# Layer 0's scatter: rows and running sums by TensorE products in place of VectorE scans, the mask by GpSimd alone, and a first pair of products from the upper rows

## The chip, the cores and the metric

The kernel runs on one core of a Trainium2 chip. The metric is the device time of one execution in microseconds. Before the change it is 974.45 us (median of three runs, 974.11 to 974.66). The engines are TensorE (PE; its weight loads are PEld), VectorE (DVE), ScalarE (ACT), GpSimd (POOL) and SyncE (SP), which issues the transfers.

## What is computed

Four graph layers follow each other on `x` of 32 x 512 x 128, with one 512 x 512 matrix `adj`. Each layer takes `h = max(layernorm(x), 0)` and adds its result to `x`. Layer 0, cut to what matters:

```python
h0 = einsum('bnf,fg->bng', input, W[0]);  h1 = einsum('bnf,fg->bng', input, W[1])
m = adj > 0
idx = cumsum(m.reshape(-1).astype(int32)) - 1
vals = e[0][idx].reshape(adj.shape)        # e has 256 entries: an index past them reads the last
A = softmax(where(m, vals, NEG), axis=1)
out = einsum('ij,bjg->big', A * M, h0) + einsum('ij,bjg->big', A * (1 - M), h1) + bias   # M = eye
```

So the first 256 positive places of `adj`, counted row by row, get their own value of `e`, and all later ones the last value. Layer 1 multiplies `h` by `adj` in several hops, layer 2 by `adj * adj`, layer 3 is an attention masked by `adj`:

```python
A = exp(tanh(Q @ K.T / sqrt(D) / 8) * 8) * A_shape;  out = (A / A.sum(-1)) @ x @ v     # A_shape = adj
```

## The kernel before

Rows are in four blocks of 128 (`NT` = 4). The 256 positions of `e` lie on the partitions in two blocks (`NK` = 2). A preparation finds, for each of the 256, its row and column, scatters their values into a 512 x 512 score by TensorE, and makes `att`, the softmax. `q` counts pairs of batches (16 of them), `r` rounds of two pairs.

```python
# ... loads: adj, x(0), x(1), w0, ecol, elast, x(2..7), b0, qw, kw, x(8..15), the rest: all issued by SyncE
for t in range(NT):                                   # mask and its row counts
    nc.vector.tensor_scalar(m[:, t, :], adj_s[:, t, :], 0.0, None, OP.is_gt, OP.add, accum_out=rc[:, t : t + 1])
for t in range(NT):                                   # 0 where there is an edge, NEG elsewhere
    nc.gpsimd.tensor_scalar(att[:, t, :], m[:, t, :], -1.0, -NEG, OP.add, OP.mult)
# ... adj transposed by 16 TensorE transposes, copied by ScalarE, stored to adjT_d for layer 3
# ... pi: number of edges up to and with each row; pc: the same, along the free axis (products with upto)
for t in range(NT):                                   # of_row[row, k]: is position k in this row?
    nc.vector.tensor_scalar(s, cols[:, :NE], incl[:, t : t + 1], None, OP.is_lt)
    nc.vector.scalar_tensor_tensor(of_row[:, t, :], cols[:, :NE], before[:, t : t + 1], s, OP.is_ge, OP.mult)
    for kk in range(NK):                              # pg: the mask row of each position
        nc.tensor.matmul(pg[kk], of_row[:, t, blk(kk)], m[:, t, :], ...)
# ... pb: edges before that row; keep_busy(6) above and keep_busy(18) here: products whose result nobody reads
for kk in range(NK):                                  # row of each position
    nc.vector.tensor_scalar(s, pc, rows[:, kk : kk + 1], None, OP.is_le, OP.add, accum_out=row_of[:, kk : kk + 1])
# ... statistics of pairs 0 and 1; ScalarE writes m * (-elast) to us[t], GpSimd adds it to att
for kk in range(NK):                                  # column of each position
    nc.vector.tensor_tensor_scan(w, pg[kk], zero.to_broadcast([P, N]), bk[:, kk : kk + 1], OP.add, OP.add)
    nc.vector.tensor_scalar(s, w, rows[:, kk : kk + 1], None, OP.is_le, OP.add, accum_out=col_of[:, kk : kk + 1])
# ... at_row, at_col, at_part: 0/1 and value matrices made from row_of and col_of by VectorE
def score_rows(t):                                    # 8 products of 512 columns per block of rows
    ...
def softmax_rows(t):
    nc.vector.scalar_tensor_tensor(u, ph, elastn, att[:, t, :], OP.mult, OP.add)
    nc.vector.tensor_tensor_reduce(u, pv, u, 1.0, 3.0e38, OP.add, OP.min, least[:, t : t + 1])
    nc.scalar.activation(u, u, AF.Exp, bias=least[:, t : t + 1], scale=-1.0, accum_out=total[:, t : t + 1])
def scaled_rows(t, u):
    nc.vector.reciprocal(total[:, t : t + 1], total[:, t : t + 1])
    nc.scalar.mul(split(att[:, t, :]), crossed(u), total[:, t : t + 1])
    # ... GpSimd takes the diagonal out of att into diag
# ... att transposed by TensorE (16 of 128 x 128), copied whole into attT, sums of its quarters for the products
```

The products of layer 0 use seven half-size products per pair in place of eight (banks `a`, `c`, `d`; `u` holds partial sums; `rt_g` and `sums_att` are the sums that they need):

```python
ORDER = ((1, "a", True), (6, "c", True), (5, "d", True), (7, "c", False), (2, "a", False),
         (4, "c", False), (3, "d", False))
```

In round `r` TensorE also makes the projections `p_g` of the pairs of the next round, from `hT`, the normed input with features on the partitions. For pairs 0 to 3 `hT` comes from TensorE transposes. From pair 4 on it goes through memory: VectorE transposes 32 x 32 blocks into `hb`, four stores bring them to `d`, one load brings `hT` back.

```python
def turn_steps(h, name, done):
    for b in range(2):
        nc.vector.transpose(hb[:, :, b].rearrange(...), h[:, b].rearrange(...))
        yield
    for i in range(NQR):
        nc.sync.dma_start(d[:, :, i, :].rearrange("j c e -> c j e"), hb[i * QR : (i + 1) * QR].rearrange(...))
    nc.sync.dma_start(hT.rearrange("p i b n -> p (i b n)"), d.rearrange("j c i e -> (j c) (i e)"))
```

Up to the end of layer 0 TensorE, VectorE, ScalarE and GpSimd run their instructions in the order of the source (`tc.manual_schedule`). SyncE isn't among the engines named there, and after layer 0 a scheduler orders all of them.

Of the kernel before, what the change touches and what calls it, by code (L numbers as in the profile page):

```python
# [24 lines left out]
def kernel(  # L25
# [95 lines left out]
    def load_rows(ap, name):  # L121
        o = ap.shape[0] // P
        w = const.tile([P, o, ap.shape[1]], F32, name=name)
        nc.sync.dma_start(w, ap.rearrange("(o f) g -> f o g", f=P))
        return w
# [9 lines left out]
    load_x(0)  # L135
    load_x(1)
    w0 = const.tile([P, 2, D], F32, name="w0")
    nc.sync.dma_start(w0, w_l0.rearrange("o f g -> f o g"))
    ecol = const.tile([P, NK], F32, name="ecol")
    nc.sync.dma_start(ecol, e_l0.rearrange("o (k p) -> p (o k)", p=P))  # L140
    elast = const.tile([P, 1], F32, name="elast")
    nc.sync.dma_start(elast, bass.AP(tensor=e_l0.tensor, offset=e_l0.offset + NE - 1, ap=[[0, P], [1, 1]]))
    for b in range(2, 8):
        load_x(b)
    b0 = load_bcast(bias_l0, "b0")
    qw = load_rows(q_w, "qw")[:, 0, :]
    kw = load_rows(k_w, "kw")[:, 0, :]
    for b in range(8, B // 2):
        load_x(b)
# [32 lines left out]
    zero = const.tile([P, 1], F32, name="zero")  # L182
    nc.vector.memset(zero, 0.0)
# [13 lines left out]
    def stats_steps(q, powers=False):  # L197
# [11 lines left out]
        if powers:  # L209
            nc.gpsimd.tensor_scalar(sd, st[:, :, :, 2], 1.0 / D, EPS, OP.mult, OP.add)  # L210
            nc.gpsimd.tensor_tensor(rs, sd, minus_half, OP.pow)
            nc.gpsimd.tensor_mul(sh, st[:, :, :, 1], rs)
            nc.gpsimd.tensor_scalar(sh, sh, -1.0, None, OP.mult)
        else:
            nc.scalar.activation(sd, st[:, :, :, 2], AF.Sqrt, bias=eps, scale=1.0 / D)
            yield
            nc.vector.reciprocal(rs, sd)
            nc.vector.scalar_tensor_tensor(sh, st[:, :, :, 1], -1.0, rs, OP.mult, OP.mult)  # L218
        shift[q] = sh.rearrange("p k e -> p (k e)")
        scale[q] = rs.rearrange("p k e -> p (k e)")  # L220
        if powers:
            yield
# [22 lines left out]
    def pe_steps(h, name, hT, copy=nc.scalar.copy):  # L245
        ps = [bank(f"p_{name}_{b}") for b in range(2)]
        for b in range(2):
            for t in range(NT):
                nc.tensor.transpose(ps[b][:, blk(t)], h[:, b, t, :], ident)
        yield  # L250
        for b, p in enumerate(ps):
            copy(hT[:, :, b, :].rearrange("p b (a c) -> p b a c", c=QR), crossed(p))
# [40 lines left out]

    def att_sums():
# [5 lines left out]
        sums["att"] = {1: a11, 2: a12, 3: s4, 4: a22, 5: s1, 6: s2, 7: a21}  # L300
        for out, p, bank_of, half, first in ((s1, a21, 2, 1, False), (s2, s1, 0, 0, False),
                                             (a21, a21, 0, 0, True), (s4, s2, 2, 0, True)):
            for k in range(2):
                b = pt[bank_of + k][:, half * H : half * H + H]
                if out is s1:
                    nc.vector.tensor_add(out[:, k], b, p[:, k])
                elif first:
                    nc.vector.tensor_sub(out[:, k], b, p[:, k])
                else:
                    nc.vector.tensor_sub(out[:, k], p[:, k], b)  # L310

# [24 lines left out]
    def products(name, form, left, right, evict):  # L336

        banks = {}
        for k, g, first in ORDER:
# [79 lines left out]
    def project_steps(q, hT, copy=nc.scalar.copy):  # L419
# [9 lines left out]
        for b in range(2):  # L429
            copy(g[r][:, :, b, w, :], pg[b])  # L430

# [14 lines left out]
    adjT = last.tile([P, NT, N], F32, tag="x", name="adjT")  # L446
# [4 lines left out]

    m = prep.tile([P, NT, N], BF16, name="m")
    rc = prep.tile([P, NT], F32, name="rc")
    for t in range(NT):
        nc.vector.tensor_scalar(m[:, t, :], adj_s[:, t, :], 0.0, None, OP.is_gt, OP.add,
                                accum_out=rc[:, t : t + 1])
    rch = prep.tile([P, NT], F16, name="rch")
    nc.vector.tensor_copy(rch, rc)


    att = square_tile("att")
    for t in range(NT):
        nc.gpsimd.tensor_scalar(att[:, t, :], m[:, t, :], -1.0, -NEG, OP.add, OP.mult)
    pt = [bank(f"p_adjT_{j}") for j in range(NT)]
    for t in range(NT):
        transpose_rows(pt, adj_s, t)
    for j in range(NT):
        nc.scalar.copy(adjT[:, j, :], pt[j])
    adjT_d = bounce.tile([N, N], F32, tag="adjT", name="adjT_d", bufs=1)
    nc.sync.dma_start(adjT_d.rearrange("(t p) w -> p t w", p=P), adjT)  # L470
# [6 lines left out]


    pi = bank("p_incl")
    for t in range(NT):  # L480
        for s in range(t + 1):
            nc.tensor.matmul(pi[:, t : t + 1], upto[:, s, blk(t)], rch[:, s : s + 1],
                             start=(s == 0), stop=(s == t))
    pc = bank("p_count")
    for t in range(NT):
        nc.tensor.matmul(pc, rch[:, t : t + 1].to_broadcast([P, P]), upto[:, t, :],
                         start=(t == 0), stop=(t == NT - 1))
    incl = prep.tile([P, NT], F32, name="incl")
    nc.vector.tensor_copy(incl, pi[:, :NT])
    before = prep.tile([P, NT], F32, name="before")  # L490
    nc.vector.tensor_sub(before, incl, rc)
    befh = prep.tile([P, NT], BF16, name="befh")
    nc.vector.tensor_scalar(befh, before, float(NE), None, OP.min)
    keep_busy(6)

    of_row = prep.tile([P, NT, NE], BF16, name="of_row")
    pb = bank("p_before")
    pg = [bank(f"p_row_{kk}") for kk in range(NK)]
    for t in range(NT):
        s = prep.tile([P, NE], F16, tag="lt", name=f"lt_{t}", bufs=2)  # L500
        nc.vector.tensor_scalar(s, cols[:, :NE], incl[:, t : t + 1], None, OP.is_lt)
        nc.vector.scalar_tensor_tensor(of_row[:, t, :], cols[:, :NE], before[:, t : t + 1], s,
                                       OP.is_ge, OP.mult)
        for kk in range(NK):
            nc.tensor.matmul(pg[kk], of_row[:, t, blk(kk)], m[:, t, :], start=(t == 0), stop=(t == NT - 1))
    for kk in range(NK):
        for t in range(NT):
            nc.tensor.matmul(pb[:, kk : kk + 1], of_row[:, t, blk(kk)], befh[:, t : t + 1],
                             start=(t == 0), stop=(t == NT - 1))
    keep_busy(18)  # L510
    row_of = prep.tile([P, NK], F32, name="row_of")
    col_of = prep.tile([P, NK], F32, name="col_of")
    at_row = prep.tile([P, NK, N], BF16, name="at_row")
    at_col = prep.tile([P, NK, N], BF16, name="at_col")
    at_part = prep.tile([P, 3, NK, N], BF16, name="at_part")

# [12 lines left out]
    elastn = prep.tile([P, 1], F32, name="elastn")  # L529
    nc.gpsimd.tensor_scalar(elastn, elast, -1.0, None, OP.mult)  # L530
    us = [prep.tile([P, N], F32, tag="u", name=f"u_{t}", bufs=NT) for t in range(NT)]

    def value(t):
        nc.scalar.mul(us[t], m[:, t, :], elastn)

    def entries(t):
        nc.gpsimd.tensor_add(att[:, t, :], us[t], att[:, t, :])

    value(0)
    value(1)  # L540
    for kk in range(NK):
        s = prep.tile([P, N], F16, tag="scr", name=f"scr_r{kk}", bufs=2)
        nc.vector.tensor_scalar(s, pc, rows[:, kk : kk + 1], None, OP.is_le, OP.add,
                                accum_out=row_of[:, kk : kk + 1])
    ln = [stats_steps(q, powers=q < 2) for q in range(4)]
    go(ln[0])
    entries(0)
    entries(1)
    go(ln[1])
    bk = prep.tile([P, NK], F32, name="bk")  # L550
    nc.vector.tensor_copy(bk, pb[:, :NK])
    for kk in range(NK):
        w = prep.tile([P, N], F32, tag="scan", name=f"scan_{kk}", bufs=1)
        nc.vector.tensor_tensor_scan(w, pg[kk], zero.to_broadcast([P, N]), bk[:, kk : kk + 1], OP.add, OP.add)
        s = prep.tile([P, N], F16, tag="scr", name=f"scr_c{kk}", bufs=2)
        nc.vector.tensor_scalar(s, w, rows[:, kk : kk + 1], None, OP.is_le, OP.add,
                                accum_out=col_of[:, kk : kk + 1])
    h = {q: normed_tile(q) for q in range(3)}
    hT = {q: feature_major(f"hT0_{q}") for q in range(4)}
    normal = [normed_steps(q, h[q]) for q in range(3)]  # L560
    copies = [nc.scalar.copy, nc.vector.tensor_copy, nc.scalar.copy]
    turned = [pe_steps(h[q], f"hT0_{q}", hT[q], copies[q]) for q in range(3)]
    project = [project_steps(q, hT[q], copies[q]) for q in range(3)]
    go(normal[0])
    next(turned[0])
    next(turned[0], None)
# [6 lines left out]
    go(normal[1], 2)  # L573
    value(2)
    value(3)
    entries(2)
    entries(3)
    go(normal[1])
# [42 lines left out]
    for t in range(NT):  # L621
        score_rows(t)
# [499 lines left out]
```

## Time and profile before

| | |
|---|---|
| time, median of 3 | 974.45 us |
| span of the profiled execution | 972.7 us |
| granted TensorE clock, mean | 0.999 |
| first product of layer 0 (`p_l_a`) starts | 37.25 us |
| round 1 starts (next `p_l_a`) | 59.95 us |
| round 2 starts | 79.18 us |
| DMA, mean over the span | 88 GB/s |

Times within the profile count from the first instruction of the span. A line of a group or of the timeline names the source line, the engine, the operation, and the tiles as out<-in, buffer numbers left out. What an engine waited for is shown as waiter <- releaser, with its total time, the number of waits and the longest. The page's own line of the granted clock, in forty slices of 24.3 us (tenths of full speed; 9 is 90% or more), reads:

```profile
PEclk9999999999999999999999999999999999999999
```

It is a mean over each slice, so a short stretch at a lower clock does not show in it.

### The profile page before, as it was taken

The page shows a single profiled execution, that of the slowest core. Times are in us where ns is not written, and L with a number is a line of the kernel's source. Part 1 is how long each engine was busy: PE and PEld are TensorE (multiplying, and loading weights), DVE is VectorE, ACT ScalarE, POOL GpSimd, SP SyncE. Part 2 cuts the span into 40 slices and gives each one's busy share as a digit, 9 for nine tenths or more (in the row PEclk, how much of TensorE's full clock was granted, in tenths as well). Part 3 has the DMA queues.
Part 4 walks back from the last instruction along what each step waited for, and adds up shares of the span by engine and source line. Part 5 has one row for each costly group of instructions (what it writes and reads, how often), then busy time and mean ns, then how long its engine had stood idle before and what let it go on. Part 6 is the DMA issues. An engine that isn't in the chain of part 4 may idle for free.

```text
span 972.7 us, 15180 instructions
## 1 busy us (share of the span) xinstructions
PE 959.0 (99%) x5474; PEld 781.9 (80%) x5474; DVE 581.0 (60%) x1316; ACT 474.6 (49%) x1058; POOL 436.5 (45%) x478
## 2 busy tenths in 40 slices
PE   7999999999999999999999999999999999999998
PEld 4799999898989989889887777777676777777776
DVE  7778896746446545646667756656554444454444
ACT  4874552452242242376628544455674455544553
POOL 5786998842436632531524443334142333223322
PEclk9999999999999999999999999999999999999999
DMA  9145643252421212344233332332131121121111
GB/s 258 52 130 152 192 112 109 66 131 65 129 88 50 82 53 57 109 109 105 71 109 109 108 87 67 87 87 75 55 91 64 44 76 55 56 75 44 55 33 44
DMA packets 82330, 86.04 MB, mean 88 GB/s; under 512 B 6737, under 2 KB 72529, under 8 KB 82257
## 3 DMA queue, kind: packets, MB, share of 16 engines
q1 hardware_dynamic: 82256, 85.09, 31.4%
q8 instruction: 43, 0.70, 0.3%
q14 instruction: 31, 0.25, 0.1%
HBM read 44.17 MB, written 40.89 MB: 87 GB/s over the span
## 4 chain that ended last, share of the span: by engine, by line
PE 91%; DVE 4%; ACT 2%; DMA 2%; SPq 1%; issue 0%; POOL 0%; DVEq 0%; ACTq 0%
PE p_av L1043 12%; PE p_score L1028 11%; PE p_l_c L356 9%; PE p_l_a L356 6%; PE p_l_d L356 6%; PE p_w L405 5%; PE p_msgT_c L349 4%; PE p_x1T_c L349 4%; PE p_feat L405 3%; PE p_hv L405 3%; PE p_msgT_d L349 3%; PE p_msgT_a L349 3%; PE p_qkh L1015 3%; PE p_l L405 3%; PE p_g L405 3%; PE p_phi L998 3%
## 5 line engine op out<-in xcount | busy, mean ns | idle before, releaser
L231 ACT ACTIVATE h<-x,sh,rs 128x128 f32<-128x128 f32 x512 | 208.9, 484 | 56.8 <-DVE sh L218 24.9
L1033 POOL TENSOR_TENSOR ex<-ex,adjTx 128x512 f32<-128x512 f32 x64 | 83.1, 1300 | 206.4 <-ACT ex L1031 206.4
L1029 ACT ACTIVATE ex<-p_score 128x512 f32<-128x512 f32 x128 | 71.9, 587 | 124.5 <-issue 113.0
L1043 PEld LDWEIGHTS p_av<-qkh_hv,ex 128*128 128x128 f32 x1024 | 118.5, 191 | 9.4 <-issue 7.4
L1043 PE MATMUL p_av<-qkh_hv,ex 128*128 128x129 f32 x1024 | 120.1, 275 | 0.8 <-POOL ex L1033 0.8
L1028 PE MATMUL p_score<-qkh_hv,hT 128*128 128x512 f32 x256 | 115.2, 593 | 0.0
L265 DVE STREAM_TRANSPOSE hb_hT<-h 128x512 f32<-128x512 f32 x120 | 81.7, 697 | 33.4 <-ACT h L231 33.1
L1033 DVE TENSOR_TENSOR ex<-ex,adjTx 128x512 f32<-128x512 f32 x64 | 45.4, 709 | 81.8 <-ACT ex L1031 81.8
L203 DVE BATCH_NORM_STATS2 bn<-x 128x6 f32<-128x256 f32 x256 | 92.4, 416 | 0.9
L1028 PEld LDWEIGHTS p_score<-qkh_hv,hT 128*128 128x128 f32 x256 | 46.2, 190 | 46.5 <-issue 45.0
L1031 ACT ACTIVATE ex<-ex 128x512 f32<-128x512 f32 x128 | 76.6, 630 | 1.9
L330 POOL TENSOR_TENSOR rt_feat<-feat,feat 128x256 f32<-128x256 f32 x16 | 11.6, 726 | 137.2 <-ACT feat L982 137.2
L330 POOL TENSOR_TENSOR rt_w<-w 128x512 f32<-128x512 f32 x16 | 20.3, 1268 | 81.5 <-ACT w L889 81.5
L405 PE MATMUL p_w<-th,x1T 128*128 128x128 f32 x256 | 49.5, 275 | 0.0
L405 PE MATMUL p_w<-th,hs 128*128 128x128 f32 x256 | 49.5, 275 | 0.0
L370 ACT COPY x1T<-p_x1T_a 128x256 f32<-128x256 f32 x16 | 5.9, 370 | 84.3 <-PE p_x1T_a L349 84.3
L405 PEld LDWEIGHTS p_hv<-vw,hT 128*128 128x128 f32 x256 | 33.6, 192 | 15.3 <-issue 8.1
L993 POOL TENSOR_TENSOR x<-x,phi2b 128x256 f32<-128x256 f32 x64 | 44.5, 728 | 0.0
L1000 ACT ACTIVATE msgT<-p_phi,phi1b 128x512 f32<-128x512 f32 x32 | 21.7, 678 | 40.7 <-PE p_phi L999 40.7
L666 POOL TENSOR_TENSOR hd<-hT,adiag 128x512 f32<-128x512 f32 x32 | 39.7, 1277 | 1.7 <-ACT adiag L779 1.7
L1048 DVE SCALAR_TENSOR_TENSOR x<-p_av,rsum,x 128x128 f32<-128x128 f32 x128 | 39.1, 347 | 1.9
L982 ACT ACTIVATE feat<-feat 128x512 f32<-128x512 f32 x32 | 20.1, 628 | 40.6 <-DVE feat L981 40.6
(231 smaller groups left out, 2084.0 us busy)
## 6 DMA issues: line engine op xcount, KB each, us to landing
d_hT<-hb_hT SPq DMA_DIRECT2D x240, 128.0 KB
hT<-d_hT SPq DMA_DIRECT2D x60, 512.0 KB
x<-in_x_dram SPq DMA_DIRECT2D x32, 256.0 KB
out_dram<-x SPq DMA_DIRECT2D x31, 256.0 KB
adj_s<-in_adj_dram SPq DMA_DIRECT2D x4, 256.0 KB
adjT_d<-adjT SPq DMA_DIRECT2D x1, 1024.0 KB
sq<-in_adj_dram SPq DMA_DIRECT2D x4, 256.0 KB
adjTx<-adjT_d SPq DMA_DIRECT2D x4, 256.0 KB
```

Source lines behind the costliest of these rows:

```text
L203: nc.vector.bn_stats(st[:, k].rearrange("p e s -> p (e s)"), xt[q][:, b, t : t + 2, :].rearrange("p t f -> p f t"))
L231: nc.scalar.activation(h[:, b, t, :], xt[q][:, b, t, :], AF.Relu, bias=shift[q][:, i : i + 1], scale=scale[q][:, i : i + 1])
L265: nc.vector.transpose(hb[:, :, b].rearrange("p j t r -> p t j r"), h[:, b].rearrange("p t (j c) -> p t j c", c=QR))
L349: nc.tensor.matmul(p[:, :H], b[:, k, :], a[:, k, :], start=(first and k == 0), stop=(k == 1), skip_group_check=True)
L356: nc.tensor.matmul(p[:, i * 2 * D : (i + 1) * 2 * D], a[:, k, blk(i)], b[:, k], start=(first and i == 0 and k == 0), stop=(k == 1), skip_g ...
L405: nc.tensor.matmul(p[:, blk(t)], hT(t), w, start=(i == 0), stop=(i == len(terms) - 1))
L993: tc.keep_in_program_order(nc.gpsimd.tensor_add(xi, xi, spread(phi2b, 2)))
L1028: nc.tensor.matmul(ps, hT[:, t, b, :], qkh, start=True, stop=True)
L1029: nc.scalar.activation(ex[:, t, :], ps, AF.Tanh, scale=1.0 / (8.0 * math.sqrt(D)))
L1031: nc.scalar.activation(ex[:, t, :], ex[:, t, :], AF.Exp, scale=8.0)
L1033: eng.tensor_mul(ex[:, t, :], ex[:, t, :], adjTx[0][:, t, :])
L1043: nc.tensor.matmul(po[:, i, : D + 1], ex[:, t, blk(i0 + i)], hv[:, t, :], start=(t == 0), stop=(t == NT - 1))
```

## The change

It is meant to shorten the preparation ahead of layer 0's first product. Its parts:

- The row of each position comes out of the same small products that give the edges before it (`known` holds, per row, the edges before it and its own number), and the running sum along a row comes from products with the triangular `upto`: first `pgs`, the transposed mask rows, then `pw = pgs x upto`. The two scans and the two counts of rows on VectorE go.
- The mask of the softmax is made by GpSimd in two operations; ScalarE no longer writes `m * (-elast)`.
- `adj` is transposed in 32 x 32 blocks by VectorE in round 1 and stored in that order; layer 3 reads it crossed. TensorE's 16 transposes go.
- `elast`, `ecol`, `qw` and `kw` are loaded by ScalarE's queue, the first four batches of `x` right after `adj`, and the statistics of pairs 0 and 1 are taken in halves.
- In round 0 the order is 1, 2, 6, 5, 7, 4, 3: products 1 and 2 need only rows 0 to 255 of `att`, that is half of each `attT` block, which is copied in halves. The other rows are transposed between them.
- GpSimd scales rows 0 to 2 of the softmax, ScalarE row 3. `keep_busy` is 8, 3, 2, 4 and 1 products instead of 6 and 18.

```diff
+    keep_busy(8)
+    def masked(t):
+        nc.gpsimd.tensor_scalar(att[:, t, :], m[:, t, :], -2.0 * NEG, NEG, OP.mult, OP.add)
+        nc.gpsimd.tensor_scalar(att[:, t, :], att[:, t, :], elastn, None, OP.max)
...
-        for kk in range(NK):
-            nc.tensor.matmul(pg[kk], of_row[:, t, blk(kk)], m[:, t, :], start=(t == 0), stop=(t == NT - 1))
+        for j in range(NT):
+            nc.tensor.matmul(pg[j // 2][:, j % 2, :], m[:, t, blk(j)], of_row[:, t, :], ...)
...
+            nc.tensor.matmul(pb[:, kk, :], of_row[:, t, blk(kk)], known[:, t, :], ...)
+    nc.scalar.copy(pgs[:, 0:2, :], pg[0])
+    nc.vector.tensor_copy(pgs[:, 2:4, :], pg[1])
+    nc.vector.tensor_copy(row_of, pb[:, :, 1])
+    nc.vector.tensor_sub(rest, rows[:, :NK], pb[:, :, 0])
+    for kk in range(NK):
+        for j in range(NT):
+            nc.tensor.matmul(pw[kk][:, j * P :], pgs[:, j, blk(kk)], upto[:, j, j * P :], ...)
...
-        nc.vector.tensor_tensor_scan(w, pg[kk], zero.to_broadcast([P, N]), bk[:, kk : kk + 1], OP.add, OP.add)
-        nc.vector.tensor_scalar(s, w, rows[:, kk : kk + 1], None, OP.is_le, OP.add,
+        nc.vector.tensor_scalar(s, pw[kk], rest[:, kk : kk + 1], None, OP.is_le, OP.add,
                                 accum_out=col_of[:, kk : kk + 1])
...
+    ORDER0 = (ORDER[0], ORDER[4]) + ORDER[1:4] + ORDER[5:]
...
+    def turn_adj():
+        ab = last.tile([P, N // QR, NT, QR], F32, tag="x", name="adj_squares")
+        for t in range(NT):
+            nc.vector.transpose(ab[:, :, t, :], adj_s[:, t, :].rearrange("p (j c) -> p j c", c=QR))
+            yield
+        for b in range(NQR):
+            tc.keep_in_program_order(nc.sync.dma_start(adjT_d[:, blk(b)]..., ab[b * QR : (b + 1) * QR]...))
+        yield
...
             elif i == 1:                       # rounds 1 to 7
                 add(0, 1, 1)
+                if r == 1:
+                    go(squares, 3)
...
             elif i == 4:
+                if r == 1:
+                    go(squares, 3)
...
-                eng.tensor_mul(ex[:, t, :], ex[:, t, :], adjTx[0][:, t, :])
+                eng.tensor_mul(split(ex[:, t, :]), split(ex[:, t, :]), crossed(adjTx[0][:, t, :]))
```

## The prediction

> **What bounds the kernel now.** I read the page's busy times first, then TensorE's waits, then three stretches of the span. Busy times, share of the span, instructions:
>
> ```profile
> PE 959.0 (99%) x5474; PEld 781.9 (80%) x5474; DVE 581.0 (60%) x1316; ACT 474.6 (49%) x1058; POOL 436.5 (45%) x478
> ```
>
> All that TensorE waited for, by its own waits (us in total, times, longest):
>
> ```profile
> PE p_adjT L444 <- DMA adj_s<-in_adj_dram: 4.7, 2, 3.8
> PE p_x1T_c L349 <- DVE x1T L372: 2.5, 7, 0.4
> ```
>
> The stretches are the preparation up to layer 0's first product, round 0, and rounds 1 and 2 (length, then busy time and count of PE, weight load, DVE, ACT, POOL; clock; DMA share; GB/s):
>
> ```profile
> 0.00:37.25 37.25, 31.32 (x171) 18.54 (x171) 28.80 (x83) 22.64 (x48) 22.09 (x44) 1.00 0.73 201
> 37.25:59.95 22.70, 22.24 (x145) 20.45 (x146) 15.31 (x38) 18.24 (x46) 16.72 (x15) 1.00 0.13 32
> 59.95:100.00 40.05, 40.05 (x250) 36.98 (x249) 35.32 (x78) 20.34 (x51) 31.37 (x26) 1.00 0.62 172
> ```
>
> From 37.25 on none of TensorE's own waits is longer than 0.6 us. So only two things move the end: when its unbroken stream begins, and any new gap in it. Before 37.25 its busy time is mostly filler (`keep_busy`); there the chain runs through VectorE. The timeline of VectorE (start, length):
>
> ```profile
> 12.27 0.74 DVE L543 TENSOR_SCALAR_CACHE_REDUCE scr_r<-p_count,rows 128x512 f16<-128x512 f32 x1
> 16.44 1.28 DVE L554 TENSOR_TENSOR_SCAN scan<-p_row,bk,zero 128x512 f32<-128x512 f32 x1
> 18.55 1.28 DVE L554 TENSOR_TENSOR_SCAN scan<-p_row,bk,zero 128x512 f32<-128x512 f32 x1
> 21.59 2.02 DVE L585 TENSOR_SCALAR at_part<-cols,col_of,part 128x512 bf16<-128x512 f16 x6
> ```
>
> The last `at_part` ends at 23.6; TensorE's 32 scatter products end at 29.05, then softmax, transposes of `att`, and copies lead to 37.25.
>
> **What the Trainium skill says.** "SBUF — State Buffer", section "SBUF: two separate sides": VectorE and GpSimd share one port pair as an exclusive lock. The trace agrees: this VectorE operation takes 0.20 us at 44.37, but beside a GpSimd add it ends only when that add ends:
>
> ```profile
> 36.92 0.82 DVE L218 SCALAR_TENSOR_TENSOR sh<-bn,rs 128x8 f32<-128x8 f32 x1
> 36.46 1.26 POOL L330 TENSOR_TENSOR rt_g<-g 128x512 f32<-128x512 f32 x1 [1.23 <-DVE g L430]
> ```
>
> "DMA: Bandwidth & Descriptors", section "Issuing engines are not separate DMA queues": moving issues to ScalarE saves issue time alone, the engines are the same. No run here shows it yet; the weights would delay `adj`. "Perfetto Trace Analysis", section "DMA Instruction — HWDGE (DVE, Sync)": an issue waits for its semaphores in the issuing sequencer, so later issues stand behind it. "TensorE: Matmul & The Clock Gate", section "Part 1: The HAM clock gate (the "warmup" mystery)": after an idle window of about 3.4 us the array runs at half rate until it has been busy as long. The start agrees: `p_idle` products of 512 columns follow at 0.43 us until 12.3, then at 0.216.
>
> **The change, part by part: the preparation.** In the built program every engine's order is the old one again from round 2 on; TensorE's from the product at 52.02 (order 4, bank c) on. So I follow the new preparation to that product. Durations are those of the rows before.
>
> - Loads: 130 KB of weights and two tiny loads run beside `adj`: at about 270 KB/us, +0.5; the row counts end at 8.9 instead of 8.2.
> - `of_row`: 4 x (0.28 + 0.48) as before, after two bn (0.7) that fit the wait for `p_incl`; it ends at 13.2, and with a GpSimd mask pair (2 x 0.62) on the lock, 13.7 (12.3 before).
> - Gone: two row scans (2 x 0.74), two scans (2 x 1.28 plus 0.15), and two reads of them (2 x 0.74). New: copy of half `pgs` 0.67, two small ones 0.3, two reads of `p_upto` 2 x 0.67. The eight bn (2.7) stay in between. TensorE's `p_upto`, 2560 columns at 0.216/512 = 1.1, lies beside bn. So 13.7 + 0.7 (bn) + 0.95 + 0.7 + 0.55 (`at_row`) + 0.7 + 1.35 + 0.55 (`at_col`) + 1.6 (`at_part`) = 20.8; lock with the other masks +0.3: 21.1, against 23.6.
> - Scatter products: 32 x 0.216 less the overlap with `at_part`: 26.7 against 29.05. hT 0.9 and two halves of p_g 1.8: 29.4. `att` rows 0 and 1 are scaled by GpSimd (0.65 + 2 x 0.46 each, 27.7), their eight transposes 0.9: 30.3; half copies 0.4: the first product at 30.8 against 37.25. That is 6.4 earlier, 2.5 of it from VectorE, the rest from asking for two rows of `att` instead of four and from no longer waiting at 33 to 38.
> - Then ScalarE is the bound: table load 1.28, copies, `adiag` 0.6, h2 3.2, hT2 1.05, h3 3.2. VectorE's statistics ahead of h2 and h3 meet the GpSimd lock, 0.5 each. h3 ends near 44.7, hT3 44.9, p_g 1.8: the product of 52.02 begins near 46.5. **Gain G = 5.5**, and round 1 begins at T = 59.95 - 5.5 = 54.4.
>
> The transpose of `adj` leaves TensorE (16 x 0.21 at the cold clock, never on the chain) and becomes 4 x 0.65 on VectorE in round 1. The crossed reading in layer 3 costs nothing: GpSimd's crossed `hd` takes 1277 ns, its straight `ex` 1300.
>
> **A new wait that I expect.** SyncE is not scheduled by hand. Its timeline before:
>
> ```profile
> 54.36 1.78 SPq L270 DMA_DIRECT2D d_hT<-hb_hT  x4
> 58.10 0.34 SPq L273 DMA_DIRECT2D hT<-d_hT  x1
> 58.49 2.08 SPq L119 DMA_DIRECT2D x<-in_x_dram  x4
> 64.25 2.48 SPq L270 DMA_DIRECT2D d_hT<-hb_hT  x4
> ```
>
> Four stores for hT4, its load (landed 61.6), the loads of x, then the stores for hT5. In the new program the first store for hT5 stands ahead of the load of hT4, and it waits for the VectorE transposes of h5. Likewise two stores for hT7 stand ahead of the load of hT6. And VectorE transposes h5 only after it has read round 1's first product. TensorE before:
>
> ```profile
> 59.95 1.89 PE L356 MATMUL p_l_a<-g,attT 128*128 128x256 f32 x8
> 61.67 1.89 PE L356 MATMUL p_l_c<-rt_g,sums_att 128*128 128x256 f32 x8
> 63.40 1.95 PE L405 MATMUL p_g<-w,hT 128*128 128x128 f32 x16
> ```
>
> p_g of quad 4 needs hT4 and is due at T + 3.45. VectorE before ended the transposes of h5 at T + 4.25 (64.2). Then one store issue 0.45, the load's issue, and 3.5 to land (58.10 to 61.59): T + 8.35. TensorE waits 8.35 - 3.45 = **4.9 us**. Part of this needs no inversion: ScalarE ends h4 at 51.4 by the chain above (after h3: 0.3, two p_g copies and two hT3 copies, 3.2) against 53.3, only 1.9 earlier, so hT4 would land at 61.6 - 1.9 = 59.7 = T + 5.3 in the old order: 1.8 of the 4.9 would be there anyway.
>
> In round 2, starting at U, the same: transposes of h7 end at U + 4.2 (83.4 - 79.18), two issues 0.9, landing 3.3 to 3.5 plus 0.2 for the stores ahead: U + 8.8 against U + 3.6 due: **5.2 us**. hT5 and hT7 are not late: hT5 lands near T + 17, due T + 18.8 after the stall.
>
> Each gap is over 3.4 us, so by the clock gate page each can end at half rate, 1.7 us lost or more, by how the window falls. I allow **0.9** for both.
>
> Sum: 974.45 - 5.5 + 4.9 + 5.2 + 0.9 = 979.95, say 980.0.
>
> **Rivals.**
> 1. The inversion costs nothing, as h5 and h7 are ready early. Against: the built program has the transposes behind the reading of the first product, and before, VectorE ran them at 62.93 and 82.16, as late as I say. Then only G is left: 969, or 970.8 with the late hT4.
> 2. The preparation gains little: the lock, or a cold TensorE, which gets 17 fillers where 24 stood, around sparse products. Cold, the scatter products take 6.9 us more. For: the old fillers were needed until 12.3; against: `p_upto`, four fillers and the transposes precede the products. G = 2 and both stalls: 983.5.
> 3. VectorE becomes the bound in round 1, since 2.6 us of transposes join the 35.3 of 40.05. Against: it catches up during TensorE's 4.9 us gap. At most 1.5 more: 981.5.
> 4. The clock drops at both gaps: 2 x 2.5: 984.
>
> **Range and chances.** I give the inversion 85%; within it G between 4 and 7 and clock losses between 0 and 4 make 976 to 984. Rival 1 takes most of the rest, below the range. The range 974.5 to 985.0 leaves about a tenth at either end. Being 2% (19.5 us) off in either direction needs three and a half times G, or more than twice the stalls: faster 0.01, same 0.96, slower 0.03.
>
> **What would show it.** Right: TensorE's first p_l_a near 31; the product of order 4 in bank c near 46.5; two waits of TensorE at p_g on DMA hT, 4 to 6 us each, about 58 and 82; on SyncE the load of hT4 right after the first store for hT5; the clock line under 9 there. From 100 us on, the same stretch lengths as before. Wrong: p_g without a DMA wait (then near 969); a first product after 33 (G was too big); a new wait in layers 1 to 3, which I hold to be unchanged.

## The result, and the profile after

The changed kernel takes 988.19 us (median of four runs, 987.01 to 988.89), the kernel before 974.28 beside it: a ratio of 1.014 (95% interval 1.0124 to 1.0159), 13.9 us slower. I had put it at 980.0, so the direction is right and the size is not.

TensorE's own waits, changed kernel (us in total, times, longest):

```profile
PE p_g L425 <- DMA hT<-d_hT: 11.6, 2, 5.8
```

It is new: the two waits that the prediction named. By stretches of the changed kernel (preparation, round 0, round 1, round 2 up to its second `p_l_a`; length, then busy time and count of PE, weight load, DVE, ACT, POOL; clock; DMA share; GB/s). The 1.00 in the first row holds only from 14.39 on, where this trace's record of the clock begins (12.28 before the change); ahead of that the first eight `p_idle` products of 512 columns take 0.45 us each, twice the 0.216 of full rate.

```profile
0.00:33.17 33.17, 26.71 (x151) 15.88 (x152) 24.94 (x75) 15.76 (x37) 25.77 (x49) 1.00 0.76 194
33.17:57.31 24.14, 23.91 (x153) 21.42 (x153) 16.28 (x42) 19.80 (x49) 19.83 (x20) 1.00 0.06 12
57.31:85.37 28.06, 22.21 (x123) 20.13 (x122) 18.52 (x43) 11.13 (x29) 15.62 (x14) 0.88 0.55 141
85.37:102.47 17.10, 11.32 (x51) 9.98 (x50) 8.04 (x22) 7.41 (x19) 10.98 (x9) 0.80 0.66 186
```

The same two last stretches of the kernel before are 19.23 and 8.70 long, with TensorE busy throughout:

```profile
59.95:79.18 19.23, 19.23 (x123) 17.78 (x121) 16.89 (x40) 10.17 (x26) 14.88 (x13) 1.00 0.62 171
79.18:87.88 8.70, 8.70 (x51) 7.87 (x50) 8.60 (x21) 5.03 (x13) 8.70 (x8) 1.00 0.79 212
```

So the preparation is 4.08 shorter (33.17 against 37.25), of which round 0 gives 1.44 back, and 2.64 is left when round 1 starts. Round 1 then loses 28.06 - 19.23 = 8.83 and the first part of round 2 loses 17.10 - 8.70 = 8.40. Together: -2.64 + 8.83 + 8.40 = +14.6, against 986.9 - 972.7 = 14.2 of the spans. Everything later cancels to 0.4.

Inside these losses stand the two waits; the rest is nearly all the clock, as an experiment below shows. TensorE and SyncE of the changed kernel there (start, length; in brackets the idle time and its releaser):

```profile
66.77 3.79 PE L425 MATMUL p_g<-w,hT 128*128 128x128 f32 x16 [5.84 <-DMA hT<-d_hT]
...
94.76 3.75 PE L425 MATMUL p_g<-w,hT 128*128 128x128 f32 x16 [5.78 <-DMA hT<-d_hT]
```

```profile
55.11 7.57 SPq L280 DMA_DIRECT2D d_hT<-hb_hT  x5
62.91 0.34 SPq L283 DMA_DIRECT2D hT<-d_hT  x1
...
79.05 3.37 SPq L478 DMA_DIRECT2D adjT_d<-adj_squares  x4
82.47 7.96 SPq L280 DMA_DIRECT2D d_hT<-hb_hT  x6
90.66 0.34 SPq L283 DMA_DIRECT2D hT<-d_hT  x1
```

Five stores ahead of hT4's load in place of four, six ahead of hT6's: the group of five lasts 7.57 us, where four took 1.78 before, as the fifth waits for VectorE. And 16 products of `p_g` take 3.79 in place of 1.95. The same stretch cut where the trace's records of the clock change it (columns as above):

```profile
57.31:65.59 8.28, 3.62 (x18) 2.85 (x16) 8.24 (x17) 4.70 (x13) 8.28 (x8) 1.00 0.37 95
65.59:72.41 6.82, 5.64 (x21) 5.27 (x22) 2.42 (x10) 2.07 (x6) 3.50 (x3) 0.50 0.80 234
72.41:92.89 20.48, 16.58 (x100) 14.86 (x98) 15.25 (x33) 7.54 (x19) 11.36 (x10) 1.00 0.53 127
92.89:99.72 6.83, 4.96 (x20) 4.72 (x21) 0.31 (x3) 1.57 (x4) 3.46 (x3) 0.50 0.80 236
```

Two stretches of 6.83 us at half rate, one per wait. The page's clock line nearly averages them away; it reads 8 in two slices:

```profile
PEclk9988999999999999999999999999999999999999
```

### The profile page after: what moved, and what is told of

Read it like the earlier page. It is cut to its first block, busy times and chain, and to the rows that moved or that the text cites. A ratio compares the mean times of both kernels' runs of the same rounds, so it can differ in the third digit from the quotient of the medians.

```text
span 986.9 us, 15155 instructions
## 1 busy us (share of the span) xinstructions
PE 961.6 (97%) x5463; PEld 784.6 (79%) x5464; DVE 578.3 (59%) x1316; ACT 469.9 (48%) x1052; POOL 443.9 (45%) x489
## 4 chain that ended last, share of the span: by engine, by line
PE 87%; POOL 4%; DVE 4%; ACT 2%; issue 1%; DMA 1%; SPq 0%; POOLq 0%; DVEq 0%; ACTq 0%
PE p_av L1107 12%; PE p_score L1092 11%; PE p_l_c L376 8%; PE p_l_d L376 5%; PE p_w L425 5%; PE p_l_a L376 5%; PE p_msgT_c L369 4%; PE p_x1T_c L369 4%; PE p_feat L425 3%; PE p_hv L425 3%; PE p_msgT_d L369 3%; PE p_msgT_a L369 3%; PE p_qkh L1079 3%; PE p_l L425 3%; PE p_g L425 3%; PE p_phi L1062 3%
## 5 line engine op out<-in xcount | busy, mean ns | idle before, releaser
L219 DVE BATCH_NORM_STATS2 bn<-x 128x6 f32<-128x256 f32 x248 | 89.7, 416 | 0.9
L1092 PEld LDWEIGHTS p_score<-qkh_hv,hT 128*128 128x128 f32 x256 | 46.2, 190 | 46.5 <-issue 45.0
L347 POOL TENSOR_TENSOR rt_feat<-feat,feat 128x256 f32<-128x256 f32 x16 | 11.6, 727 | 137.2 <-ACT feat L1046 137.2
L425 PE MATMUL p_g<-w,hT 128*128 128x128 f32 x256 | 34.7, 294 | 11.6 <-DMA hT<-d_hT 11.6
L450 ACT COPY g<-p_g 128x512 f32<-128x512 f32 x30 | 17.4, 584 | 56.6 <-PE p_g L425 56.4
L425 PEld LDWEIGHTS p_g<-w,hT 128*128 128x128 f32 x256 | 33.4, 209 | 12.6 <-DMA hT<-d_hT 6.2
```

The lines of the kernel that those rows point to most:

```text
L219: nc.vector.bn_stats(st[:, k].rearrange("p e s -> p (e s)"), xt[q][:, b, t : t + 2, :].rearrange("p t f -> p f t"))
L425: nc.tensor.matmul(p[:, blk(t)], hT(t), w, start=(i == 0), stop=(i == len(terms) - 1))
L1092: nc.tensor.matmul(ps, hT[:, t, b, :], qkh, start=True, stop=True)
```

## The experiments

The theory A to be tested: SyncE's order makes both waits and the waits make the half clock. Against it B: hT4 and hT6 are late for other reasons (ScalarE's h4, other transfers). Besides, for the clock, C against another cause; for the small gain of the preparation, D (TensorE's own stream is the bound) against D' (GpSimd).

### The order alone, put into the kernel before

```diff
+            if name == "hT0_5" and i == 0:
+                yield            # the first store for hT5 is issued here, the other three after hT4's load
```

(SyncE kept in program order for these; no other engine's order moves.)

> The kernel before, with the inversion alone put in on SyncE: the first store for hT5 stands ahead of the load of hT4; every other engine's order and all of the preparation are the old ones. Theory A: the store waits for VectorE's transposes of h5 (they end near 64.2), the load then lands near 68.3, p_g is due at 63.4, so TensorE waits about 5 us; then a stretch at half clock costs about 2.5 more: 974.4 + 5 + 2.5 = 982. Theory B (order alone makes no wait, only the new preparation's late h4 and transfers do): no wait of TensorE above 0.6, 974.4.

Measured: 981.66 us (981.12 to 982.38), ratio 1.0075 (1.0058 to 1.0092). TensorE of this kernel:

```profile
68.25 3.76 PE L410 MATMUL p_g<-w,hT 128*128 128x128 f32 x16 [5.16 <-DMA hT<-d_hT]
71.80 2.72 PE L361 MATMUL p_l_d<-rt_g,sums_att 128*128 128x256 f32 x8
```

A wait of 5.16, and products at half rate behind it. One store in the wrong place of SyncE's order costs 7.2 us in an otherwise unchanged kernel (974.45 beside it). A stands, B falls as the main cause.

### The old order of SyncE in the changed kernel

```diff
+        kept = tc.keep_in_program_order if name.startswith("hT0_") else lambda i: i
-            nc.sync.dma_start(d[:, :, i, :]..., hb[i * QR : (i + 1) * QR]...)
+            kept(nc.sync.dma_start(d[:, :, i, :]..., hb[i * QR : (i + 1) * QR]...))
```

> The changed kernel, in which SyncE alone issues in another order: the loads of hT4 and hT6 stand ahead of every store for hT5 and hT7, as in the kernel before; no other engine's order moves. Theory A (the inversion on SyncE makes both waits, and the waits make the half clock): the last store for hT4 landed at 58.78 and a load takes 3.5, so hT4 is there near 62.3 and TensorE waits 1.5 us in place of 5.8; the last store for hT6 landed at 88.05, so hT6 is there near 91.5 and the wait is 2.7 in place of 5.8 (the stores of the transposed adj still go ahead of hT6's own). Both gaps stay under 3.4, so no stretch at half clock: 988.2 - 4.3 - 3.1 - 5.3 = 975.5. Theory B (hT4 and hT6 are late anyway, through ScalarE's h4 and through other transfers): both waits stay near 5 to 6 us, 986 to 988.

And besides, adj's stores behind the load of hT6:

```diff
+                if A + 4 < NQ:
+                    go(turn(A + 4))
                 if r == 1:
                     go(squares, 3)
-                if A + 4 < NQ:
-                    go(turn(A + 4))
```

> The same as the kernel with only SyncE's order put back, and besides the turn of pair 6 stands ahead of the last step of adj's transpose, so that the stores of the transposed adj go behind the load of hT6. Theory A, with these stores as the cause of what is left at hT6: the wait near 89 falls from about 2.7 to under 0.5, the one near 61 stays at 1.5; 972.8 us, 2.7 less than with SyncE's order alone. Rival (hT6 is late by VectorE's own transposes of h6, not by the stores ahead): the wait near 89 stays above 2, the time within 0.5 of the other.

Measured: 978.39 (ratio 1.0043, 1.0028 to 1.0058) and 978.46 (1.0043, 1.0026 to 1.006). The first kernel's two waits:

```profile
62.48 2.05 PE L426 MATMUL p_g<-w,hT 128*128 128x128 f32 x16 [1.32 <-DMA hT<-d_hT]
...
84.64 3.41 PE L426 MATMUL p_g<-w,hT 128*128 128x128 f32 x16 [2.65 <-DVE bn L219]
```

(The second line names a `bn` of VectorE that ended at 84.56, but `p_g` doesn't read it; the load of hT6, which it does read, was issued at 81.15 and landed at 84.50.) The waits are what A said, 1.32 for 1.5 and 2.65 for 2.7, and 9.8 us of the 13.9 come back. But the times are 2.9 and 5.7 over the expectations. In the first kernel 1.5 of this is a stretch at half clock after a gap of only 2.65 us, which I had held to be safe: 3.41 us long, 84.14 to 87.56. In the second kernel the wait at hT6 goes, but the one at hT4 is 2.05, and hT7 becomes late by 2.39, again with a half-rate stretch of 3.41. The stores of `adj` move the delay; they don't stop making it.

### Work for TensorE inside the gaps

```diff
+        for _ in range(fill):    # 20 ahead of p_g of pairs 4 and 6, overwritten by it
+            nc.tensor.matmul(p[:, blk(0)], ones, ones, start=True, stop=True)
```

> The changed kernel with 20 extra products (128 columns, FP32, about 4.4 us, their result overwritten) on TensorE ahead of the projections of pairs 4 and 6, inside both gaps; SyncE's inversion stays. Theory C (the half clock comes from the gaps): TensorE is idle for some 1.5 us at each place in place of 5.8, no stretch at half clock follows, p_g takes 1.8 and not 3.6, and the time falls by 2.8 + 2.5 to about 983. Rival (the clock falls for another reason, such as the load of the chip at these times): both stretches of 6.83 us stay, 988.

Measured: 983.86 us (983.52 to 984.55), ratio 1.0099 (1.0084 to 1.0114). Its first gap:

```profile
60.88 4.63 PE L424 MATMUL p_g<-ones 128*128 128x128 f32 x40
66.86 2.05 PE L427 MATMUL p_g<-w,hT 128*128 128x128 f32 x16 [1.34 <-DMA hT<-d_hT]
```

The data come as late as before (66.86 for 66.77), the clock stays full, here and at the second gap, and `p_g` takes 2.05. So 4.3 us of the loss is the clock (4.9 between the two profiled spans), made by the gaps: C.

### GpSimd relieved in the preparation

```diff
-        nc.gpsimd.tensor_scalar(att[:, t, :], m[:, t, :], -2.0 * NEG, NEG, OP.mult, OP.add)
+        nc.gpsimd.tensor_scalar(far, m[:, t, :], -2.0 * NEG, NEG, OP.mult, OP.add)       # far: BF16
-    scaled_rows(0)
+    scaled_rows(0, nc.scalar.mul)                                                       # and row 1
```

> The changed kernel with GpSimd relieved ahead of the first product: the mask's intermediate is a BF16 tile (it was FP32, 1.57 us an operation), and rows 0 and 1 of the softmax are scaled by ScalarE. Rows 0 and 1 of att are then there some 3 us earlier. Theory D (TensorE's own stream sets the first product: scatter products, then 8 transposes of h and 32 products of the projections, 3.6 us): the first p_l_a moves by less than 0.3 from 33.17, round 1 by less than 0.3 from 57.31, 988. Theory D' (GpSimd's 1.57 us operations, which I had counted at 0.65, set it): the first p_l_a near 31.5, round 1 near 55.7, 986.5.

Measured: 987.26 us (986.71 to 988.1), ratio 1.0135 (1.012 to 1.0151). The BF16 tile changes nothing, the operation still takes 1.57; but with ScalarE's scaling (0.72 each) row 1 of `att` is ready at 29.80 in place of 31.85. The first `p_l_a` starts at 33.37, no earlier; round 1 at 57.04. D' falls: GpSimd was close behind, not the bound. The seven kernels traced with the changed kernel's preparation start round 1 between 57.26 and 57.66, so the 0.27 is hardly more than their scatter.

### All four rows ahead of the first product

```diff
     transpose_rows(pt, att, 1)
+    transpose_rows(pt, att, 2)
+    transpose_rows(pt, att, 3)
```

(and taken away behind the first product).

> The changed kernel with TensorE alone reordered: all 16 transposes of att ahead of the first product, as in the kernel before, while the scatter stays the new one. It takes away the part that asks for two rows first. GpSimd ends row 3 of att at 35.4, so the first p_l_a comes near 36.2 in place of 33.17; the second product then follows at once (no transposes between), near 38 in place of 35.95. If TensorE's stream then is the bound, all that follows moves by 1.9 to 2.4: round 1 near 59.4, 990.3; that is nearly the 59.95 of the kernel before, and the new scatter by itself gained about half a microsecond. By the sum of my prediction (the two rows worth 3.9, kept to the end) round 1 comes near 61, 992. Rival (ScalarE hides it): round 1 within 0.5 of 57.31, 988.5.

Measured: 991.68 us (991.58 to 991.96), ratio 1.0181 (1.0165 to 1.0196), 3.5 over the changed kernel; round 1 starts at 60.01. TensorE:

```profile
34.54 0.66 PE L465 MATMUL p_attT<-ident,att 128*128 128x128 f32 x4 [1.49 <-POOL att L653]
35.49 0.66 PE L465 MATMUL p_attT<-ident,att 128*128 128x128 f32 x4 [0.29 <-POOL att L653]
36.28 1.99 PE L376 MATMUL p_l_a<-g,attT 128*128 128x256 f32 x8
```

The first product is where I expected it, the second is 1.1 later than I expected (39.15, it waits 0.88 for VectorE's `u_l`). Round 1 then starts as in the kernel before (60.01 against 59.95). So of the 2.64 all or nearly all (2.4 to 2.7, by the scatter named above) comes from asking for two rows first, and the new scatter, in which GpSimd makes the rows, gains nothing without it.

### The stores of adj spread, and the projection later

```diff
-                    go(squares, 3)                # round 1: last transpose and all four stores
+                    go(squares, 1)                # round 1: last transpose
+                if r in (2, 3):
+                    go(squares, 1)                # one store behind each of the loads of hT7 to hT10
```

> The changed kernel with SyncE's order put back, and the four stores of the transposed adj spread: one behind the load of hT7, hT8, hT9 and hT10 each, in rounds 2 and 3, in place of all four in round 1. No other engine's order moves. If these stores (0.85 us each of SyncE, ahead of those for hT6 or hT7) made the waits of 2.65 and 2.39 that the two kernels with the order put back still had: only the 1.3 to 2.0 us at hT4 stays, no stretch at half clock, and round 2 starts 0.6 to 1 earlier than in the kernel before: 974.4 - 2.4 + 1.7 = 973.7. Rival (x and hT's own stores are late by themselves, since rounds follow each other 2.4 earlier): a wait over 2 us at p_g of pair 6 or 7 stays, 976 or more.

```diff
+            elif i == 2 and r == 1:               # was at i == 1
+                go(projection(A + 2))
```

> The same as the kernel with the stores of the transposed adj spread, and besides the projections of pair 4 one product later in round 1 (1.73 us), so that hT4, which lands 1.3 to 2.0 after its place, is there or nearly. Theory A holds all the loss to be these waits and their clock: then only the gain of the preparation is left, 974.4 - 2.4 + 0.3 = 972.3, faster than both kernels. Rival: another wait comes in its place (the projection's bank, or g for round 2), 973.7 or more.

Measured: 974.62 (973.43 to 977.72; ratio 1.0008, 1.0 to 1.0017) and 973.53 (972.95 to 974.61; ratio 0.9997, 0.9988 to 1.0005). In the first, hT6 and hT7 are in time and the wait at hT4 (1.30) is the only one left in its trace, that of the fastest of twelve runs: the stores of `adj` were the rest. In the second, hT4's wait is gone, but I had not foreseen two others: 0.97 for VectorE's `u_l`, behind three transposes of `adj`, and 1.55 at the projection of pair 11, where a store of `adj` and then the loads of x stand close ahead of that pair's own stores; that these made it late is argued. Level with the kernel before, 1.2 short of what I expected.

### The transpose of adj moved as well

```diff
-                if r == 1:
-                    go(squares, 3)                # VectorE's transposes between the products of round 1
+                if r in (1, 2):
+                    go(squares, 2)                # two at the end of round 1, two at the end of round 2
+                if r == 3:
+                    go(squares)                   # all four stores behind the load of hT9
```

> The changed kernel with SyncE's order put back, the projections of pair 4 one product later, and the transpose of adj moved: two of its four VectorE steps at the end of round 1, two at the end of round 2, all four stores in round 3 behind the load of hT9. In the two kernels with spread stores three waits were left: 1.3 at hT4 (projection in its old place), 0.97 at u_l of round 1 (VectorE, behind three of these transposes), 1.55 at hT11 (a store and the loads of x in one stretch). With all three gone only the gain of the preparation is left: 974.0 - 2.4 + 0.2 = 971.8, faster than both kernels. Rival: VectorE or SyncE gives one of them back in another round, 973 or more.

> The same as the kernel with the transpose of adj moved, with GpSimd relieved in the preparation (BF16 intermediate of the mask, rows 0 and 1 scaled by ScalarE). That alone brought round 1 forward by 0.27 in the profile: 971.5, within 0.6 of the other.

Measured: 972.65 (972.42 to 974.14), ratio 0.9986 (0.9978 to 0.9995), and with GpSimd relieved 972.21 (971.9 to 973.01), ratio 0.9979 (0.997 to 0.9987). Both beat the kernel before; from each other they can't be told. Rounds 1 and 2 of the first one, up to round 3:

```profile
57.62:77.16 19.54, 19.54 (x122) 17.90 (x121) 18.81 (x42) 11.18 (x29) 15.71 (x14) 1.00 0.64 188
77.16:96.40 19.24, 19.24 (x123) 17.79 (x122) 17.91 (x39) 9.96 (x24) 14.89 (x13) 1.00 0.59 162
```

TensorE is busy throughout again. With the losses out, the preparation's gain stands alone in the time: 1.7 to 2.1 us.

### Less work for TensorE ahead of the first product

Both kernels leave out the projection of pair 1 on TensorE, so pair 1 gets no result of its own; all copies and later products stay.

```diff
+        if q == 1:               # 2 products of 512 columns in FP16 for 16 of 128 in FP32
+            for p in pg:
+                nc.tensor.matmul(p, upto[:, 0, :P], upto[:, 0, :], start=True, stop=True)
```

In the changed kernel with GpSimd relieved:

> The changed kernel with GpSimd relieved as before, and on TensorE the 16 projection products of pair 1 (0.112 us each, 1.79) left out: two FP16 products of 512 columns (0.43) stand in their place, so that 1.36 us of TensorE's stream ahead of the first product is gone and pair 1's result is not the reference's. Theory D (TensorE's stream is the bound from the scatter to round 1): first p_l_a 33.37 - 1.36 = 32.0, round 1 57.04 - 1.3 = 55.7, 985.9. Rival (ScalarE's h2 and h3, as in my prediction, is the bound behind the first product): first p_l_a near 32.0, but round 1 within 0.4 of 57.04, 987.

And in the fastest kernel:

> The fastest kernel so far (SyncE's order put back, projections of pair 4 later, adj's transpose moved, GpSimd relieved) with the 16 projection products of pair 1 left out as before, two FP16 products in their place: 1.36 us less of TensorE ahead of the first product, and pair 1's result is not the reference's. With the waits still in, the half clock hid what this is worth in the time: round 1 began 1.34 earlier, the median did not fall. Here no wait stands in its way. Theory D: round 1 at 57.11 - 1.34 = 55.8, time 972.2 - 1.3 = 970.9. Rival (the earlier start runs into hT4 or hT6, or into ScalarE): a wait of 1 us or more at p_g of pair 4, 5 or 6, time within 0.4 of 972.2.

Measured: 987.61 (986.8 to 987.69; ratio 1.0135, 1.0121 to 1.0149) in the first, where round 1 starts at 55.70, 1.34 earlier, as D says. The time does not follow: from the first late `p_g` to the next `p_l_a` it is 8.28 us in this profile and 6.83 in that of the kernel it is compared with, since the half-rate stretch began at 64.56, near the end of the gap, in place of 62.78, in its middle. In the fastest kernel there is no gap, and the time does follow: 970.51 (970.34 to 971.16), ratio 0.9966 (0.9952 to 0.9979), 1.7 less (1.4 when each is taken from the kernel before that ran beside it), with round 1 at 55.62 for 57.11. So TensorE's own work ahead of the first product is worth its whole length. But these two kernels don't show D for the whole way to round 1: ScalarE waits for TensorE's `p_adiag` (1.52 us in both, and in the two that they are compared with) before it makes h2 and h3, so the cut moves ScalarE's chain by as much, and the rival as I had put it could not come true.

## Why the prediction was wrong

Its sum was -5.5 + 4.9 + 5.2 + 0.9 = +5.5. The trace has -2.64 + 5.84 + 5.78 + 5.6 = +14.6 (the 5.6 is what the two losses, 17.2, have beyond the waits). Term by term:

- **The inversion: right.** Both waits are at the named place with the named releaser, 5.84 and 5.78 us. The single store put into the old kernel shows it for the first. Also right: about 1.8 of the first would be there in the old order; 1.3 to 2.05 was.
- **The waits 4.9 and 5.2: 1.5 short together.** At hT4 the step "VectorE ended the transposes of h5 at T + 4.25" failed. VectorE of the changed kernel:

```profile
59.38 1.16 DVE L228 SCALAR_TENSOR_TENSOR sh<-bn,rs 128x8 f32<-128x8 f32 x1
60.46 0.68 DVE L789 TENSOR_TENSOR u_l<-p_l_a,b 128x512 f32<-128x512 f32 x1
61.06 1.29 DVE L275 STREAM_TRANSPOSE hb_hT<-h 128x512 f32<-128x512 f32 x2
59.24 1.27 POOL L347 TENSOR_TENSOR rt_g<-g,rt_g 128x512 f32<-128x512 f32 x1
```

  The small `sh` took 1.16 there and 0.33 in the kernel before, and ends (60.54) with the GpSimd operation of the last line (60.51); the transposes end 0.8 later than I took over from the old timeline. That is the shared lock of VectorE and GpSimd (the Trainium skill, "SBUF — State Buffer", section "SBUF: two separate sides") that I had shown myself and then left out of this step. At both places the load also took longer to land than the 3.3 to 3.5 I took: 3.8 at hT4, and 4.0 at hT6 (issued at 90.66, landed at 94.63). And a second cause lies hidden beside that wait, which the prediction overlooked: `adj`'s four stores (3.37 us of SyncE) stand ahead of the stores for hT6. With the order put back a wait of 2.65 was left, and none with these stores spread.
- **The clock, 0.9: the largest error, 5.6 measured.** The step was "1.7 us lost or more, by how the window falls. I allow 0.9 for both". Both gaps of nearly 6 us cost a stretch of 6.83 us at half rate; with the gaps filled 4.3 us of the time came back. The prediction's own fourth rival had 2 x 2.5; I gave it no weight in the sum.
- **The gain, 5.5: 2.64 measured.** The sign that I had named for this, a first product after 33, came (33.17 for 30.8). VectorE's part came nearly as worked out, the last `at_part` ends at 21.23 for 21.1, in part by luck: `at_part` takes 2.02, as its line had shown, and not the 1.6 of the sum. Of the 2.9 missing, 2.4 are lost by the first product. The step that failed is "two halves of p_g 1.8": it counts 16 products, but there are 32 (28.43 to 32.00, 3.57 us).

```profile
28.43 3.74 PE L425 MATMUL p_g<-w,hT 128*128 128x128 f32 x32
```

  The scatter products, too, end 0.9 later (27.56 for 26.7), 0.46 of it a wait for ScalarE's copy of `hT`. Behind the first product, "Then ScalarE is the bound" holds in the main. ScalarE there:

```profile
38.88 0.58 ACT L833 COPY adiag<-p_adiag 128x512 f32<-128x512 f32 x1 [1.45 <-PE p_adiag L832]
39.36 3.19 ACT L239 ACTIVATE h<-x,sh,rs 128x128 f32<-128x128 f32 x8
44.19 3.19 ACT L239 ACTIVATE h<-x,sh,rs 128x128 f32<-128x128 f32 x8 [0.35 <-DVE sh L228]
```

  It waits for `p_adiag`, so it starts as late as TensorE does; the eight transposes of `att` that no longer stand ahead of the first product now stand ahead of `p_adiag`. Then come h2 and h3, and TensorE's transposes of h3 take 2.14 in place of 1.04, since h3 arrives piece by piece. In all twelve traced kernels with the new preparation round 1 starts 13.1 us after h3 begins. h3 ends at 47.38 for the 44.7 worked out, 2.7 later, when the first product is 2.4 later.

  A small third error: GpSimd's operations with a value per partition take 1.57, for the 0.65 (scaling) and 0.62 (mask) assumed. It cost at most 0.3 here, as TensorE was later still; where four rows are asked for first, TensorE waits for these rows (the 1.49 above). The gain is near rival 2's 2 us, but not by its cause: the clock is full from 14.39 on, ahead of the scatter products (19.49 to 27.56).
- **What I held to be unchanged was:** layers 1 to 3 cancel to 0.4 us.

The three errors, 4.7, 2.9 and 1.5, all point the same way, so nothing cancels. Three slips in the working change nothing here: the fillers number 18, not 17; 44.9 + 1.8 makes 46.7, not 46.5; and by its own terms the inner range is 977.5 to 984.5, not 976 to 984.

Not tried: four rows first with ScalarE scaling them all, which would tell what the new scatter is worth by itself; nor less work for ScalarE behind `p_adiag`, which would tell D from the prediction's own account of round 0.

## What to carry to other kernels

Where one queue carries both the stores of the next block and the load of this one, look at its order in the built program and not at the source: a load that stands behind one store waits for all that the store waits for, here 5 to 6 us. Price a gap of TensorE together with the clock behind it, half as much again here (5.6 beside 11.6). And when an engine's first product is to come earlier, count that engine's own work ahead of it, instruction by instruction: 16 products left out of the count took 1.8 us of the gain.

## What the runs showed that I had not expected

The half clock needs no idle time as long as its window. The changes lie on a grid of 3.41 us (65.59, 72.41, 92.89, 99.72 in the changed kernel are 2, 6 and 2 windows apart); the Trainium skill, "TensorE: Matmul & The Clock Gate", section "Part 1: The HAM clock gate (the "warmup" mystery)", says that this window runs free, and the trace agrees. But the table of that section has the half rate follow an idle window, and here, with the old order put back, a gap of 2.65 us was enough, of which 2.16 fell into the window that ended at 84.14:

```profile
80.73:84.14 3.41, 1.25 (x6) 0.76 (x4) 3.41 (x9) 2.13 (x6) 3.41 (x4) 1.00 0.57 175
84.14:87.56 3.42, 2.92 (x14) 2.95 (x15) 1.73 (x6) 0.58 (x1) 3.42 (x4) 0.50 1.13 314
```

TensorE was busy 1.25 of 3.41 us in it. Gaps of 2.05 (split by a window's edge), 1.3 and 1.55 left the clock alone. With all fourteen traces cut into the windows of their own grids, from 20 to 950 us, one picture comes out. Each of the eleven full-rate windows in which TensorE was idle for 2.12 us or more was followed by half rate, and none in which it was idle for 1.83 or less; no window lay between. The two nearest, of the changed kernel with GpSimd relieved and of the same with less work for TensorE:

```profile
59.37:62.78 3.41, 1.29 (x6) 0.78 (x5) 3.41 (x6) 2.41 (x7) 3.41 (x4) 1.00 0.00 0
57.74:61.15 3.41, 1.58 (x8) 1.04 (x6) 3.39 (x5) 2.13 (x6) 3.41 (x3) 1.00 0.00 0
```

The way back needs more work than staying: a half-rate window with 0.50 us idle (84.14 above) was the last at half rate, one with 0.73 was not:

```profile
64.56:67.97 3.41, 2.68 (x12) 2.69 (x13) 1.19 (x4) 0.57 (x1) 2.94 (x3) 0.50 1.18 313
```

Each of the nine gaps of 5.2 to 6.0 us in these traces cost two windows at half rate, and those of 2.39 and 2.65 one.

How the grid lies to the program differs from trace to trace, which would explain why kernels with gaps scatter more (976.6 to 980.5 in one); that is argued, not shown.

GpSimd's `tensor_scalar` on 128 x 512 took 0.62 with two constants (FP16 input) and 1.57 with a value per partition, with an FP32 and a BF16 input alike. GpSimd of the kernel with GpSimd relieved:

```profile
22.13 0.62 POOL L519 TENSOR_SCALAR far<-m 128x512 bf16<-128x512 f16 x1
22.85 1.57 POOL L520 TENSOR_SCALAR att<-far,elastn 128x512 f32<-128x512 bf16 x1
```
